# Fewer TensorE products, ScalarE marks and moved input tests in a two-layer graph attention kernel

## The chip, the cores and the metric

The kernel runs on one core of a Trainium2 chip. The metric is the device time of one execution in microseconds: 2030.03 us, the median of three runs (2026.96 to 2030.07).

## What is computed

There are 4096 nodes with 512 features and a dense 0/1 matrix `adj` (4096 x 4096). Layer 0 is attention over all pairs with 8 heads of 64; layer 1 is attention inside blocks of 128 nodes. Cut to what matters:

```
feats = einsum('nf,hfo->hno', x, W)
d = s_self[:, :, None] + s_neigh[:, None, :]
d = where(d > 0, d, 0.2 * d) * adj
x = layernorm(x + relu(softmax(d) @ feats + b))
scores = (where(mask, q @ k.T * scale, 0) + adj + adj) * where(mask, 1, -1e6)
x = layernorm(x + softmax(scores) * mask @ v)
```

`mask` is true inside a block of 128 nodes. A zero of `adj` makes the logit 0, and its exponential 1, so every pair counts in the softmax.

## The kernel before

The function `adjacency_streamed_path` does the work; `general_path` runs only if a flag computed from the inputs asks for it, and doesn't in these runs. Because the logit is a sum of a row part and a column part, exp of it is a product of vectors per node. Write E for the unmasked exponential after the leaky step, scaled by column; then A E + (1 - A) is summed against the features.

**Passes and steps.** Layer 0 goes in four passes `r` of two heads each. A pass has four chunks `c` of 1024 rows, and a chunk has 32 steps `j` of 128 columns. At a step, VectorE makes for each of the two heads a tile `q` (128 x 1024): max of a row tile and a scalar, times the adjacency tile `at` (line 1560). TensorE multiplies `q` by scaled features `g_s` into the sum `acc` (line 1607), and multiplies `at` by minus the plain features `f_s` into the sum `accf` (line 1584), in two parts of a split number: 4 matmuls for each step. From `q` a 0/1 tile `mark` is made, which tells which branch of the leaky step applied: on ScalarE by a steep sigmoid (line 1570), but for every fourth step's second head on VectorE by a comparison (line 1565). Every eight steps, TensorE sums the marks into `dens` (line 1623), from which denominators come.

**Folded steps.** `folded(j)` names steps in which A (E - 1) is made by VectorE itself, in two operations instead of one (lines 1548 and 1551), with a row `U_row` and a scalar `c_all`, its mark always on ScalarE (line 1555). Then `q` goes into `accf`, and the 4 matmuls of line 1584 fall away. In the kernel before, 36 of 512 steps are folded: 12 in pass 0, 4 in pass 1 (chunk 2), none in pass 2, 20 in pass 3.

**Groups and buffers.** In passes 0 to 2 a group is eight steps: TensorE does the group's `accf` products, then its `acc` products, then the marks' sums. Eight `q` buffers serve there (six in pass 3), so VectorE runs at most four steps ahead. At the end of a chunk `sums_to_rows` (line 1268) scales the sums on VectorE and later turns them into rows, in pieces put between groups (`run_pieces`).

**Layer 1.** In pass 3 and after it, blocks of 512 rows go through `layer_1` (line 1079), a generator that yields after each stretch of work; letters in `PLANS` and in the last line's string say which generator goes on: E the turned sums of a chunk and `rows_of_layer_0`, F the norm, R the second block's rows, a and b the two blocks in work, K the flag. Within a block: transposes to `x1T` (copied out of PSUM by ScalarE, line 1086), products to `zT` (line 1105, copied at 1112), scores (1132), exponentials on ScalarE (1157), values (1180), output products (1196), the norm and the output. `rows_of_layer_0` loads `x1b` and, per tile, `hp`, the earlier passes' output, through a pool of two buffers.

**The 0/1 tests.** `check_block` takes one of 128 tiles `ck` of `adj` (128 x 1024) through two ScalarE operations (Square, then Abs with a sum, lines 1248 and 1249), which show whether all its values are 0 or 1. The tiles have two buffers; `load_block` queues the next load on SP when one is done. They run in passes 1 to 3, one for each four steps and a second one every third time.

**What sets the order.** TensorE's order is that of the program (`manual_schedule`). The other engines' queues are ordered by the framework's planner, but for instructions pinned by `keep_in_program_order`, among them the first half of each test. [...]

Of the kernel before, what the change touches and what calls it, by code (L numbers as in the profile page):

```python
# [19 lines left out]
P = 128  # L20
# [384 lines left out]
def adjacency_streamed_path(  # L405
# [55 lines left out]

    g_d = dram.tile([PR, NT // 4, P, 4 * FP], F32, name="g_d")
    f_d = dram.tile([PR, NT // 4, P, 4 * 2 * FP], F32, name="f_d")
    FOLDED = (0, 1, PR - 1)
    FOLDS = {1: {4: (1,), 5: (0, 1), 6: (0, 1, 2)}, 2: {2: (1,), 4: (1,), 5: (0, 1), 6: (0, 1, 2)}, 3: {2: (1,), 4: (1,), 5: (0, 1), 6: (0, 1, 2)}}
    pu_d = dram.tile([3 * H, N], F32, name="pu_d")
    at_d = dram.tile([NCH, NT, P, C], F32, name="at_d")
    hs_d = dram.tile([N, FP * (PR - 1)], F32, name="hs_d")
# [468 lines left out]
        columns_of_exponentials(NB - 1, misc([P, 4, 2 * H]))  # L937

    ckp = ctx.enter_context(tc.tile_pool(name="ck", bufs=2))
    psa = ctx.enter_context(tc.tile_pool(name="ps_acc_f", bufs=1, space=PSUM))  # L940
    dens = psa.tile([P, HB], F32, name="dens")
    nc.vector.memset(dens, 0.0)
# [136 lines left out]
    def layer_1(blk, x1b, lp, lp1, lp2):  # L1079
# [91 lines left out]
        yield  # L1171
        vs = {}

        def values(u, split=FC, pv=None):
            if pv is None:
                pv, fs = misc([P, F]), range(split)
            else:
                fs = range(split, FC)
            for f in fs:
                nc.tensor.matmul(  # L1180
                    pv,
                    x1T[:, f, ts(u, P)],
                    L1["wvT"][:, f, :],
                    start=(f == 0),
                    stop=(f == FC - 1),
                )
            if fs[-1] == FC - 1:
                vs[u] = lp.tile([P, F], F32, name="v_t")
                nc.vector.tensor_add(vs[u], pv, L1["bv"])
            return pv  # L1190

        def rows_out(us):
            ys = []
            for u in us:
                po = misc([P, F])
                nc.tensor.matmul(po, pT[:, u, :], vs[u], start=True, stop=True)  # L1196
                y = lp.tile([P, F], F32, name="y_f")
                nc.vector.scalar_tensor_tensor(
                    y, po, rd[:, u : u + 1], x1b[:, u, :], op0=OP.mult, op1=OP.add
                )  # L1200
                ys.append(y)
            layernorm(ys)()
            for i, u in enumerate(us):

                queue = nc.sync if blk >= NT // 4 - 2 else nc.gpsimd
                queue.dma_start(out[ts(4 * blk + u, P), :], ys[i])

        values(0)
        pp = misc([P, 4, P])
# [8 lines left out]
        values(2)  # L1218
        if blk == NT // 4 - 1:
            last = values(3, 3)  # L1220
            rows_out((2,))
            values(3, 3, last)
            yield
            rows_out((3,))
        else:
            values(3)
            yield
            rows_out((2, 3))
# [24 lines left out]
    def rows_of_layer_0(blk, hst, lp):  # L1253
        x1b = lp.tile([P, 4, F], F32, name="x1b")
        for u in range(4):
            it = 4 * blk + u
            nc.sync.dma_start(x1b[:, u, :], x[ts(it, P), :])
            hp = lp.tile([P, F - FP], F32, name="hp_l")
            nc.sync.dma_start(hp, hs_d[ts(it, P), :])
            for dst, src in (  # L1260
                (x1b[:, u, : F - FP], hp),
                (x1b[:, u, F - FP :], hst[:, it % CT, :]),
            ):
                nc.vector.scalar_tensor_tensor(dst, src, 0.0, dst, op0=OP.max, op1=OP.add)  # L1264
        plan["F"] = layernorm([x1b[:, u, :] for u in range(4)])
        return x1b

    def sums_to_rows(r, c, acc, accf, ae, u_row, later_by):
# [178 lines left out]
    def main_pass(r, ae=None, wide=4):  # L1447
# [9 lines left out]
        for c in range(NCH):  # L1457
# [5 lines left out]
            def folded(j):  # L1463

                if r == PR - 1:
                    return r in FOLDED and c > 0 and j % 4 in FOLDS[c].get(j // 4, ())
                if r == 1:
                    return c == 2 and j in (8, 16, 24, 25)
                return r in FOLDED and j % 8 == 0 and j > 0

            def rows_for_folded():
# [32 lines left out]
                            stop=(j >= NT - 2),  # L1504
                        )

            acc = psa.tile([P, 2, HB], F32, name="acc")
            accf = psa.tile([P, 2, HB], F32, name="accf")
            marks = {}
            for j0 in range(0, NT, wide):  # L1510
# [30 lines left out]
                for j in cycle:  # L1541
                    for h in range(2):
                        hh = 2 * r + h
                        q = qs[j, h] = ring("q", qp, 6).tile([P, C], F32, name="q")
                        d_j = d_all[:, j, hh : hh + 1]
                        if folded(j):
                            cn = c_all[r][:, j, h : h + 1]
                            nc.vector.scalar_tensor_tensor(
                                q, p_row[h], d_j, U_row[h], op0=OP.max, op1=OP.mult
                            )  # L1550
                            nc.vector.scalar_tensor_tensor(  # L1551
                                q, q, cn, ats[r, c, j].bitcast(F32), op0=OP.subtract, op1=OP.mult
                            )
                            mark = marks[j, h] = sgp.tile([P, C], FP8, name="mark")
                            nc.scalar.activation(  # L1555
                                mark, q, AF.Sigmoid, bias=below_0, scale=2.0**80, saturate=False
                            )
                            continue
                        with following(at_step == 0, ("DVE", 3 if j else 2)):
                            ends_of_setup["Q"] = nc.vector.scalar_tensor_tensor(  # L1560
                                q, p_row[h], d_j, ats[r, c, j].bitcast(F32), op0=OP.max, op1=OP.mult
                            )
                        mark = marks[j, h] = sgp.tile([P, C], FP8, name="mark")
                        if j % 4 == 3 and h == 1:
                            nc.vector.tensor_scalar(  # L1565
                                mark, q, d_j, None, op0=OP.is_gt, saturate=False
                            )
                        else:
                            with following(at_step == 0, "ACT", "ROW"):
                                nc.scalar.activation(  # L1570
                                    mark,
                                    q,
                                    AF.Sigmoid,
                                    bias=nb_all[:, j, hh : hh + 1],
                                    scale=BIG,
                                    saturate=False,
                                )
# [3 lines left out]
                for j in cycle:  # L1581
                    for w in range(0 if folded(j) else 2):
                        for s in range(2):
# [4 lines left out]
                                start=(j == 0 and w == 0),  # L1588
                                stop=(j == NT - 1 and w == 1),
                            )  # L1590
                if at_step == 0:
                    columns_of_last()
                if r == 0 and (c, j0 + wide) == (NCH - 1, NT):

                    sums_over_a(c, cycle)
# [6 lines left out]
                for j in cycle:  # L1602
                    dst = accf if folded(j) else acc
                    for s in range(2):
                        for o in range(0, FP, 32):
                            h = o // FH
                            nc.tensor.matmul(  # L1607
                                dst[o : o + 32, s, :],
                                g_s[j // 4][:, j % 4, h, o % FH : o % FH + 32],
                                qs[j, h][:, ts(s, HB)],  # L1610
                                start=(j == 0),
                                stop=(j == NT - 1),
                                skip_group_check=folded(j),
                            )
                if r == 0:
                    pieces(c, j0 // 4, 1)

# [15 lines left out]
                    pieces(c, j0 // 4, 1)  # L1633
                for x_ in follow[first:]:
                    bring(*x_)
                group_0 = (at_step - NT * NCH) // 4
                for group in range(group_0, group_0 + wide // 4) if r else ():
                    if group == 0:
                        load_block()
                        load_block()  # L1640
                    for _ in range(1 + (group % 3 == 2)):
                        check_block(done[0])
                        done[0] += 1
                        load_block()
            ends.append(sums_to_rows(r, c, acc, accf, ae, u_row, 0.75 * wide))

    done = [0]
    keep = ctx.enter_context(tc.tile_pool(name="keep_f", bufs=1))
    wide_passes = ExitStack()
    more["at"], more["q"] = [(atp, 6)], [(qp, 6)]  # L1650
# [3 lines left out]
    with tc.tile_pool(name="ps_ae", bufs=1, space=PSUM) as psx:  # L1654
        ae = psx.tile([P, HB], F32, name="ae")
        nc.vector.memset(ae, 0.0)
        banks.append(psx)
        main_pass(0, ae, wide=8)
        banks.remove(psx)
    first_pass.close()  # L1660
    banks.extend([ctx.enter_context(tc.tile_pool(name="ps_misc2", bufs=2, space=PSUM))] * 2)
    with tc.tile_pool(name="wl1", bufs=1, side="right") as wp:
        pools["wl1"] = wp
        work.append(weights_of_layer_1(keep, wp))
# [4 lines left out]
            for _ in gen:  # L1669
                pass  # L1670
        work.clear()
    main_pass(2, wide=8)
    more.clear()
    wide_passes.close()
    with tc.tile_pool(name="lp", bufs=2) as lp, tc.tile_pool(
# [2 lines left out]
        pools.update(lp=lp, lp1=lp1, lp2=lp2)  # L1678
        main_pass(3)
        plan["K"] = kind_of_inputs(lp1)  # L1680
        run_plan("bbEbbFbaabRaFaKKbbababaababbbb", pinned=True)


@with_exitstack
# [50 lines left out]
```

## Time and profile before

| | |
|---|---|
| median of the runs | 2030.03 us |
| the profiled execution | 2029.65 us |
| its span, first to last instruction | 2027.9 us |
| granted TensorE clock, mean | 0.996 |
| HBM read and written over the span | 298 GB/s |
| set-up until pass 0 begins | about 156 us |
| pass 0 | to about 568 us |
| pass 1, pass 2 | to about 949 and 1327 us |
| pass 3, then the end part | to about 1891 and 2028 us |

The boundaries are the starts of the first scaling (line 1277) after a pass. A profile names an instruction by line, engine and tiles; a group's row gives busy time, the mean of one in ns, and the idle time before it with what ended it. TensorE is PE (its weight loads PEld), VectorE DVE, ScalarE ACT, GpSimd POOL, and SP the queue that issues most loads. Of the queues, SP carried 430.64 MB at 60.9% of the 16 engines' time. Over the span ScalarE waited 25.7 us for `ck` loads, 19 times, and SP's queue, in pass 3's stretch from 1430 to 1905 us, 99.6 us for ScalarE to finish tests before their buffers could be loaded again.

### The profile page before, as it was taken

Reading aid. Unit: us, or ns where it says so; the run is one execution under the profiler, and the core shown is the slowest. Engines: PE = TensorE matmul, PEld = TensorE weight load, DVE = VectorE, ACT = ScalarE, POOL = GpSimd, SP = SyncE. Lnnn points to the kernel's source line nnn. Section 1 sums busy time; section 2 is a strip of 40 time slices with the busy share of each in tenths; the row PEclk is TensorE's granted clock in tenths of the full one; section 3 lists DMA queues with packets and bytes.
Section 4 is the critical chain, followed back from the end, with each engine's and each line's share of the span. In section 5 each row is a group of like instructions: output and inputs, shape, how many; then the busy total and the mean of one; then the engine's idle time right before and its main releaser. Section 6 shows DMA issues by size and latency. Waiting matters only on the chain. (4 is left out here: it accounts for less than half of the span.)

```text
span 2027.9 us, 38096 instructions
## 1 busy us (share of the span) xinstructions
PE 1999.2 (99%) x14961; PEld 1023.0 (50%) x14961; DVE 1756.0 (87%) x2212; ACT 1524.7 (75%) x1872; POOL 231.2 (11%) x362
## 2 busy tenths in 40 slices
PE   9999999999999999999999999999999999999997
PEld 8884454545444444445445444444444444445443
DVE  5668999999999999898999999999997897899754
ACT  3348888888879898889889899999786666567420
POOL 1222222222200000000000000000020210211111
PEclk9999999999999999999999999999999999999998
DMA  6999999999999999799999899989976775775211
GB/s 210 248 328 270 296 283 277 287 292 295 323 368 342 364 343 327 257 340 310 317 318 333 304 347 334 333 280 366 320 255 197 243 246 163 233 278 161 73 55 44
DMA packets 209673, 555.74 MB, mean 274 GB/s; under 512 B 25068, under 2 KB 66412, under 8 KB 209484
## 3 DMA queue, kind: packets, MB, share of 16 engines
q1 hardware_dynamic: 145132, 430.64, 60.9%
q0 software_dynamic: 62272, 122.04, 23.4%
q8 instruction: 120, 1.97, 0.4%
q10 hardware_dynamic: 2080, 0.52, 0.1%
q14 instruction: 69, 0.57, 0.1%
HBM read 496.11 MB, written 107.35 MB: 298 GB/s over the span
## 5 line engine op out<-in xcount | busy, mean ns | idle before, releaser
L1560 DVE SCALAR_TENSOR_TENSOR q<-p_row,d_all,at 128x1024 f32<-128x1024 f32 x952 | 1154.9, 1277 | 94.2 <-PE acc L1607 38.4
L1570 ACT ACTIVATE mark<-q,nb_all 128x1024 fp8e4<-128x1024 f32 x824 | 907.6, 1148 | 137.9 <-DVE q L1560 126.9
L1607 PE MATMUL acc<-q,g_s 128*32 128x512 f32 x7616 | 841.9, 593 | 1.2 <-DVE q L1560 0.4
L1607 PEld LDWEIGHTS acc<-q,g_s 128*32 128x32 f32 x7616 | 248.5, 110 | 556.3 <-issue 495.5
L1584 PE MATMUL accf<-at,f_s 128*128 128x512 f32 x1904 | 464.3, 399 | 2.8 <-ACT at L625 2.7
L1584 PEld LDWEIGHTS accf<-at,f_s 128*128 128x128 f32 x1904 | 351.4, 189 | 109.2 <-issue 26.3
L1248 ACT ACTIVATE ck<-ck,neg_half_f 128x1024 f32<-128x1024 f32 x128 | 146.0, 1140 | 26.0 <-DMA ck<-in_adj_dram 25.7
L1249 ACT ACTIVATE ck<-ck,neg_quarter 128x1024 f32<-128x1024 f32 x128 | 146.4, 1144 | 1.9
L1555 ACT ACTIVATE mark<-q,below 128x1024 fp8e4<-128x1024 f32 x72 | 81.6, 1145 | 78.4 <-DVE q L1551 77.9
L1623 PE MATMUL dens<-mark,e_b 128*6 128x512 fp8e4 x2048 | 125.9, 379 | 1.8 <-DVE mark L1565 1.6
L807 PE MATMUL ps_fe<-w_sb_f,xT_f 128*128 128x264 f32 (+1 forms) x512 | 121.7, 395 | 1.0 <-ACT xT_f L727 1.0
L625 ACT CAST at<-ps_m 128x1024 fp32r<-128x1024 fp8e4 x124 | 117.2, 1026 | 0.0
L1180 PE MATMUL ps_m<-wvT,x1T 128*128 128x512 f32 x256 | 114.4, 594 | 0.0
L1105 PE MATMUL ps_m<-x1T,M_sb 128*128 128x512 f32 x256 | 113.0, 595 | 0.3 <-ACT x1T L1086 0.3
L807 PEld LDWEIGHTS ps_fe<-w_sb_f,xT_f 128*128 128x128 f32 x512 | 100.6, 200 | 15.7 <-ACT xT_f L727 1.8
L1371 POOL DMA_DIRECT2D hs_d<-hst x12 | 10.7, 896 | 827.6 <-DVE hst L1361 814.5
L626 POOL DMA_DIRECT2D at_d<-at x128 | 71.0, 555 | 269.9 <-ACT at L625 141.8
L1565 DVE TENSOR_SCALAR mark<-q,d_all 128x1024 fp8e4<-128x1024 f32 x128 | 95.9, 749 | 5.0 <-PE accf L1584 0.5
L1623 PEld LDWEIGHTS <-e_b 128*6 128x6 bf16 x2048 | 55.8, 86 | 79.3 <-issue 37.1
L1551 DVE SCALAR_TENSOR_TENSOR q<-q,c_all,at 128x1024 f32<-128x1024 f32 x72 | 90.5, 1274 | 0.0
L1105 PEld LDWEIGHTS ps_m<-x1T,M_sb 128*128 128x128 f32 x256 | 47.9, 190 | 59.6 <-issue 57.8
L1180 PEld LDWEIGHTS ps_m<-wvT,x1T 128*128 128x128 f32 x256 | 47.6, 190 | 56.4 <-issue 55.2
(209 smaller groups left out, 1315.3 us busy)
## 6 DMA issues: line engine op xcount, KB each, us to landing
at<-at_d SPq DMA_DIRECT2D x384, 512.0 KB, 6.0
at_d<-at POOLq DMA_DIRECT2D x128, 512.0 KB, 17.4
ck<-in_adj_dram SPq DMA_DIRECT2D x128, 512.0 KB, 5.5
f_s<-f_d SPq DMA_DIRECT2D x107, 512.0 KB, 7.5
g_s<-g_d SPq DMA_DIRECT2D x128, 256.0 KB, 5.8
f_d<-fst POOLq DMA_DIRECT2D x16, 1024.0 KB, 7.9
a_b<-in_adj_dram POOLq DMA_DIRECT2D x32, 512.0 KB, 21.1
p_row<-pu_d SPq DMA_DIRECT2D x32, 512.0 KB, 6.7
```

The costliest lines, as they stand in the source:

```text
L625: ends_of_setup["ACT"] = nc.scalar.copy(at, both[:, :, k])
L807: nc.tensor.matmul(pf[:, q, :, cols], tile_j(xTs[k][:, c].rearrange("p u n -> p (u n)"), u), w_sb[:, c, 4 * q : 4 * q + 4, cols], start=(c ...
L1105: nc.tensor.matmul(pz, L1["M"][:, f, ts(c, P)], x1T[:, f, :], start=(f == 0), stop=(f == FC - 1),)
L1180: nc.tensor.matmul(pv, x1T[:, f, ts(u, P)], L1["wvT"][:, f, :], start=(f == 0), stop=(f == FC - 1),)
L1248: tc.keep_in_program_order(nc.scalar.activation(ck, ck, AF.Square, bias=neg_half))
L1249: nc.scalar.activation(ck, ck, AF.Abs, bias=neg_quarter, accum_out=binp[:, k : k + 1])
L1560: ends_of_setup["Q"] = nc.vector.scalar_tensor_tensor(q, p_row[h], d_j, ats[r, c, j].bitcast(F32), op0=OP.max, op1=OP.mult)
L1565: nc.vector.tensor_scalar(mark, q, d_j, None, op0=OP.is_gt, saturate=False)
L1570: nc.scalar.activation(mark, q, AF.Sigmoid, bias=nb_all[:, j, hh : hh + 1], scale=BIG, saturate=False,)
L1584: nc.tensor.matmul(accf[:, s, :], f_s[j // 4][:, j % 4, w, :], ats[r, c, j][:, ts(s, HB)], start=(j == 0 and w == 0), stop=(j == NT - 1 an ...
L1607: nc.tensor.matmul(dst[o : o + 32, s, :], g_s[j // 4][:, j % 4, h, o % FH : o % FH + 32], qs[j, h][:, ts(s, HB)], start=(j == 0), stop=(j ...
L1623: nc.tensor.matmul(dens[lo : lo + 6, :], e_b[:, j, 2 * r + h, :], marks[j, h][:, ts(s, HB)], start=(j == 0), stop=(j == NT - 1),)
```

## The change

- Folded steps: 18 more, in passes 1 (14 in place of 4) and 2 (8 in place of none); each chunk there now loads its two `U_row` rows.
- Marks: in passes 1 and 2 all marks are made on ScalarE; passes 0 and 3 keep every eighth mark on VectorE.
- Tests: 20 in each of passes 1 and 2 (42 before), 63 given out in pass 3 (44), and 25 between the steps of the end part (none). A table, `CHECKS`, names how many follow each group; in the end part one or two follow each letter of the plan. The flag (K) is computed later.
- Five small moves: `columns_of_last` comes after the first `acc` products; `acc` and a scratch bank get PSUM pools of their own; `hp` of tiles 2 and 3 uses the buffers of `v_t`; the last block's norm is done in two halves; in the last block, the third tile's output product comes ahead of the end of the fourth tile's values.

```diff
-    FOLDED = (0, 1, PR - 1)
+    FOLDED = tuple(range(PR))
+    MIDDLE_FOLDS = {(1, 0): (16, 24), (1, 1): (8, 16, 24), (1, 2): (8, 9, 16, 17, 24, 25), (1, 3): (8, 16, 24)}
...
+    psq = ctx.enter_context(tc.tile_pool(name="ps_acc_q", bufs=1, space=PSUM))
+    banks.append(ctx.enter_context(tc.tile_pool(name="ps_misc1", bufs=1, space=PSUM)))
     psa = ctx.enter_context(tc.tile_pool(name="ps_acc_f", bufs=1, space=PSUM))
...
             last = values(3, 3)
+            outputs((2,))
+            values(3, 3, last, True)
             rows_out((2,))
-            values(3, 3, last)
             yield
...
-            hp = lp.tile([P, F - FP], F32, name="hp_l")
+            hp = lp.tile([P, F - FP if u < 2 else F], F32, name="hp_l" if u < 2 else "v_t")
+            hp = hp[:, : F - FP]
...
-        plan["F"] = layernorm([x1b[:, u, :] for u in range(4)])
+        n = 2 if blk == NT // 4 - 1 else 4
+        ends = [layernorm([x1b[:, u + v, :] for v in range(n)]) for u in range(0, 4, n)]
...
-                if r == 1:
-                    return c == 2 and j in (8, 16, 24, 25)
+                if r:
+                    return j in MIDDLE_FOLDS.get((r, c), (16, 24))
...
-            acc = psa.tile([P, 2, HB], F32, name="acc")
+            acc = psq.tile([P, 2, HB], F32, name="acc")
...
-                        if j % 4 == 3 and h == 1:
+                        if j % 4 == 3 and h == 1 and r in (0, PR - 1):
...
-                if at_step == 0:
-                    columns_of_last()
...
+                if at_step == 0:
+                    columns_of_last()
...
-                group_0 = (at_step - NT * NCH) // 4
-                for group in range(group_0, group_0 + wide // 4) if r else ():
-                    if group == 0:
-                        load_block()
-                        load_block()
-                    for _ in range(1 + (group % 3 == 2)):
-                        check_block(done[0])
-                        done[0] += 1
-                        load_block()
+                if at_step == NT * NCH:
+                    load_block()
+                    load_block()
+                check_blocks(CHECKS[r, c][j0 // wide] if r else 0)
...
+    CHECKS = {(1, 0): (1, 1, 1, 1), (1, 1): (1, 1, 1, 1), (1, 2): (1, 2, 1, 2), (1, 3): (1, 2, 1, 2)}
+    CHECKS.update({(2, c): (1, 1, 1, 2) for c in range(NCH)})
+    CHECKS[3, 0] = (0, 1, 1, 0, 1, 1, 0, 1)
+    CHECKS[3, 1] = CHECKS[3, 3] = (2, 2, 2, 2, 2, 2, 3, 3)
+    CHECKS[3, 2] = (2, 3, 2, 3, 3, 3, 3, 3)
+
+    def check_blocks(n):
+
+        for _ in range(min(n, N * N // (P * CK) - done[0])):
+            check_block(done[0])
+            done[0] += 1
+            load_block()
...
-        run_plan("bbEbbFbaabRaFaKKbbababaababbbb", pinned=True)
+        for k in "bbEbbFbaabRaFabbababaa":
+            run_plan(k, pinned=True)
+            check_blocks(2 if k in "EF" else 1)
+        assert done[0] == N * N // (P * CK)
+        run_plan("babKbKbb", pinned=True)
```

## The prediction

> **What bounds the kernel now.** I read the page's busy times first, then the busy times by stage, then TensorE's waits, and then the timelines of the places that the change touches.
>
> ```profile
> span 2027.9 us, 38096 instructions
> PE 1999.2 (99%) x14961; PEld 1023.0 (50%) x14961; DVE 1756.0 (87%) x2212; ACT 1524.7 (75%) x1872; POOL 231.2 (11%) x362
> ```
>
> TensorE lacks 28.7 us of the span. A busy TensorE need not be the bound, so I look at the stages (pass 1, pass 2, pass 3, and the end part from 1891 us):
>
> ```profile
> 568.00:949.00 381.00, 379.44 (x3069) 183.44 (x3062) 352.84 (x353) 330.99 (x351) 3.60 (x4) 1.00 0.94 329
> 949.00:1327.00 378.00, 378.00 (x3141) 182.41 (x3139) 350.45 (x334) 340.42 (x358) 3.54 (x4) 1.00 0.92 325
> 1327.00:1891.00 564.00, 560.66 (x3738) 266.31 (x3738) 507.27 (x673) 408.21 (x521) 70.73 (x88) 1.00 0.71 243
> 1891.00:2028.00 137.00, 121.69 (x470) 60.55 (x468) 71.85 (x180) 28.57 (x74) 20.95 (x51) 0.96 0.17 60
> ```
>
> Columns: stretch, then busy PE, PEld, DVE, ACT, POOL, granted clock, DMA share, GB/s. In passes 1 and 2 TensorE has no gap, VectorE has 7% left and ScalarE 10 to 13%. In pass 3 ScalarE has 28% left; in the end part it is nearly free, but TensorE idles there for 15 us, so that work hangs on short chains. The few waits of TensorE itself:
>
> ```profile
> PE ps_m L1085 <- DVE x1b L525: 1.8, 1, 1.8
> PE ps_m L614 <- DVE pu_all L794: 1.6, 1, 1.6
> PE dens L1623 <- DVE mark L1565: 1.6, 1, 1.6
> ```
>
> **Folded steps: the gain.** The trace of before has chunks with unfolded, once and twice folded groups of eight steps (pass 1, chunk 2), so the saving can be read from start to start:
>
> ```profile
> 761.35 7.61 PE L1584 MATMUL accf<-at,f_s 128*128 128x512 f32 x32
> 768.88 13.94 PE L1607 MATMUL acc<-q,g_s 128*32 128x512 f32 x128
> ...
> 784.48 6.68 PE L1584 MATMUL accf<-at,f_s 128*128 128x512 f32 x28
> 790.99 0.60 PE L1334 MATMUL ps_m<-ident_f,dcs 128*128 128x128 f32 x4
> ...
> 838.41 5.80 PE L1584 MATMUL accf<-at,f_s 128*128 128x512 f32 x24
> 844.05 7.03 PE L1033 MATMUL ps_m<-w_k,w_q 128*128 128x512 f32 x16
> ```
>
> 32 matmuls take 7.53 us, 28 take 6.51, 24 take 5.64: about 0.97 us less for each folded step. 18 steps more (10 in pass 1, 8 in pass 2) give 18 x 0.97 = 17.4 us, all on the path, as TensorE has no gap there. The built program's order agrees: 28 or 24 such matmuls stand in these groups where 32 or 28 stood, and nothing else changes on TensorE but two moved pieces.
>
> **What the fold and the marks cost VectorE.**
>
> ```profile
> L1560 DVE SCALAR_TENSOR_TENSOR q<-p_row,d_all,at 128x1024 f32<-128x1024 f32 x952 | 1154.9, 1277 | 94.2 <-PE acc L1607 38.4
> L1570 ACT ACTIVATE mark<-q,nb_all 128x1024 fp8e4<-128x1024 f32 x824 | 907.6, 1148 | 137.9 <-DVE q L1560 126.9
> L1565 DVE TENSOR_SCALAR mark<-q,d_all 128x1024 fp8e4<-128x1024 f32 x128 | 95.9, 749 | 5.0 <-PE accf L1584 0.5
> ...
> 1200.37 8.46 DVE L1560 SCALAR_TENSOR_TENSOR q<-p_row,d_all,at 128x1024 f32<-128x1024 f32 x7
> 1208.93 0.75 DVE L1565 TENSOR_SCALAR mark<-q,d_all 128x1024 fp8e4<-128x1024 f32 x1
> 1212.05 10.85 DVE L1560 SCALAR_TENSOR_TENSOR q<-p_row,d_all,at 128x1024 f32<-128x1024 f32 x9 [2.37 <-PE acc L1607]
> ```
>
> In a row, q's come every 1.21 us (10.85 / 9). A folded step needs two more, 2.41 us; the two marks that leave a group give 1.34 us back. So a once folded group is 1.07 us longer on VectorE and 0.97 shorter on TensorE. An ordinary group has 2.37 us idle before its fifth step, the one that waits for q buffers: 0.3 us are left, so nothing is lost. The tightest is the group at j = 8, where VectorE also turns the last chunk's sums: its idle time there is 0.93 us, plus about 0.37 us by which the last q of a group leads TensorE. In chunk 1 of pass 1 it is folded: I charge 0.6 us. In chunks 2 and 3 weights of layer 1 lengthen TensorE's groups and cover it (idle 2.8 and 3.0 us); in pass 2 j = 8 isn't folded.
>
> Here a rule speaks against the change: the Trainium skill, "ScalarE: Activation LUTs", section "Rules for kernel authors", gives simple elementwise work to VectorE, as the faster engine. The rows agree on the price (749 against 1148 ns): 64 marks cost 64 x 0.4 = 25.5 us more engine time. By the rule alone I would forecast a loss. By the stage rows VectorE is the engine without room and ScalarE gets room: 32 marks x 1.06 us (its pace in a row) = 34 us in, and in pass 2 42 checks become 20, 22 x 2.3 = 51 us out; in pass 1 the same. Its load falls to about 325 us of 370. I take the rows: no cost. Each check now stands behind a group's last mark, where the next marks have most slack.
>
> **Loads.** Passes 1 and 2 gain seven pairs of row loads (512 KB each, 7 MB) on SP's queue and lose 44 checks' loads (23 MB): no cost. A row load waits for the folded step of the chunk before, long done; the adjacency loads stand behind it.
>
> **Small moves.** The columns of the last block of exponentials (columns_of_last) put behind the first `acc` products: removes the 1.6 us wait on pu_all, but the same copy may hold a bank a little later; 1.0 of 0 to 1.6. Loading `hp` for tiles 2 and 3 into v_t's buffers: these loads no longer wait for tiles 0 and 1, so the late mark at 1656 us goes: 1.6 (0 to 1.6). PSUM pools regrouped: same number of banks, 0 (within 1 either way). The last block's norm in two halves and its y pulled forward belong to the end.
>
> **Checks in pass 3.** 62 in place of 44 there: 18 x 2.3 = 41 us into 156 us of idle ScalarE. Copies x1T and zT keep their places behind at most two checks, as some already do; TensorE's other products cover them. 0, with a bound of 5 us.
>
> **Checks in the end part: the cost.** Here no mark and no attention product is left to hide behind. ScalarE takes its queue in order; its order in the built program puts 26 checks between the copies, one half check between most of the four x1T copies of a block. A check is 2.31 us (1901.99 to 1904.30). There are two ck buffers: load k+2 starts when check k is done. The last four of them landed as in the first line below (the others show block 6's x1T copies and TensorE around them):
>
> ```profile
> DMA to landing us min/median/max: 3.7/4.5/4.6
> ...
> 1937.37 2.08 ACT L1086 COPY x1T<-ps_m 128x512 f32<-128x512 f32 x4 [12.06 <-PE ps_m L1085]
> 1938.61 1.88 PE L1196 MATMUL ps_m<-v_t,a 128*128 128x512 f32 x4
> 1940.33 13.90 PE L1105 MATMUL ps_m<-x1T,M_sb 128*128 128x512 f32 x32
> ```
>
> DMA is quieter in the end part (share 0.17), so 4.1 us, and 0.3 for the semaphores: two checks per 2.3 + 4.4 = 6.7 us. On before's clock: check 104 (counted from 0) follows the exponentials, which end at 1923.1, and ends at 1925.4; 106 starts at 1929.8, 108 at 1936.5. The first x1T copy of block 6 then ends at 1939.4, not 1937.9; check 110, between the third and fourth, waits for its load until 1943.2; the fourth ends at 1944.9. TensorE wants it at 1940.33: 4.6 us late. Next the last zT sits behind check 115 (1962.0): total shift 3.9, since the 1.8 us wait on x1b's norm is covered now. Block 7's copies have checks 116 and 117 among them; 117's load lands at 1967.6, the last copy ends at 1969.3: shift 7.7. Last, zT behind check 124 frees its PSUM bank at 1995.5, wanted at 1992.4: shift 11.1. The y pulled forward gives 0.6 back: 10.5 us net. SP's queue carries these loads too: block 7's x1b rows and the output writes stand behind ck loads that wait for ScalarE; by the same times they come 2 to 5 us later than before, still ahead of need.
>
> The skill's "DMA: Bandwidth & Descriptors", section "Anatomy of one DMA", gives 2.0 us and bytes/436e3 (fitted on GpSimd's path): 3.2 us for 512 KB, an estimate. About 12 round trips, of which nine tenths reach the end, would then take 0.9 x 12 x 0.9 = 10 us less, and the end part would cost nothing. No ck load of the trace landed in under 3.7 us in that stretch, so I stay with 4.1.
>
> **Sum**, against the profiled execution (2029.65 us, 0.4 below the median): -17.4 + 0.6 - 1.0 - 1.6 + 10.5 = -8.9, so 2020.8; I say 2021.
>
> **Rivals.** (1) *The end part hides the checks*: for it, ScalarE's 28.6 us of work in 137. Then also the 1.8 and 0.6 us go: -22 us, 2008. (2) *VectorE becomes the bound in passes 1 and 2*: its reserve in a folded group is only 0.3 us; if half the saving is eaten, 2029.5, no change. Against it: the once folded group at 816 us shows no wait. (3) *Slower: the round trip of a check's load in the end part*. At the page's median landing of 5.5 us each of 12 trips is 1.4 us longer: 0.9 x 12 x 1.4 = 15 us more, 2036. It decides from a landing of about 5.4 us, where the end part's cost passes 24 us. For it: busy stretches show 5.5 and more; against it: the DMA share of 0.17.
>
> **Numbers.** Differences over 0.2% (4 us) can be told from none. Forecast 0.48 (2013 to 2027), (1) 0.20, (2) 0.17, (3) 0.15. Faster 0.71, same 0.16, slower 0.13. Range 2008 to 2034.
>
> **What would show it.** Passes 1 and 2 shorter by 9 and 7.5 us with TensorE at 100%; pass 3 unchanged; an end part some 10 us longer, TensorE waiting there on x1T and zT copies, ScalarE on ck loads. TensorE waiting on q would be rival 2; ck landings over 5 us, rival 3; no such waits, rival 1. I am wrong if pass 3 lengthens by more than 5 us, that is if marks or adjacency loads come late there.

## The result and the profile after

The changed kernel takes 2035.34 us, the median of 20 runs (2030.19 to 2039.00); the kernel before took 2030.84 in 20 runs taken with them. The ratio is 1.0018, 95% interval [1.0011, 1.0025]: slower by about 3.7 us by the ratio (4.5 by the medians). The interval excludes 1, but by the ratio the difference is just inside the 0.2% that I had called no change. I had forecast 2021. The profiled execution took 2031.69 us with a span of 2029.9, 2.0 us more than before's span; it lies near the bottom of its kernel's runs, which matters below.

The page of the changed kernel, as before: span, then busy time by engine.

```profile
span 2029.9 us, 38082 instructions
...
PE 1990.8 (98%) x14889; PEld 1015.4 (50%) x14889; DVE 1753.2 (86%) x2187; ACT 1610.2 (79%) x1936; POOL 220.3 (11%) x364
```

TensorE has 72 matmuls and 8.4 us of busy time less, and the span is longer: it is idle for 39.1 us where it was idle for 28.7. Where, the busy times by stage show. The stages are cut here at the start of the first `acc` product of passes 1, 2 and 3 and of the last group; the columns are as in the prediction.

```profile
577.40:971.70 394.30, 387.78 (x3153) 184.41 (x3152) 365.94 (x357) 341.83 (x334) 3.59 (x4) 0.99 0.90 305
971.70:1336.10 364.40, 364.40 (x3073) 171.38 (x3072) 341.86 (x312) 328.82 (x316) 3.54 (x4) 1.00 0.89 301
1336.10:1886.10 550.00, 548.01 (x3581) 263.18 (x3580) 493.14 (x665) 430.21 (x559) 61.78 (x92) 1.00 0.76 260
1886.10:2029.90 143.80, 119.56 (x455) 59.72 (x454) 67.18 (x170) 86.48 (x151) 19.20 (x50) 0.94 0.47 152
```

Cut the same way, before had 395.0, 371.9, 551.0 and 130.3 us. So pass 2 gained 7.5 us, as forecast; pass 1 gained 0.7 in place of 9; the end part lost 13.5 in place of 10. In pass 1 and in the end part TensorE now has gaps, and the granted clock is under 1. Its largest waits name the places (total, times, longest):

```profile
PE ps_m L1036 <- DVE parts L1352: 3.7, 1, 3.7
...
PE ps_m L1088 <- DVE mv_f L519: 2.7, 1, 2.7
PE ps_m L1183 <- ACT zT L1115: 2.1, 1, 2.1
PE ps_m L1200 <- ACT x1T L1089: 2.1, 2, 1.6
...
PE ps_m L1077 <- ACT wvT L1078: 1.8, 1, 1.8
```

The first is new and stands in pass 1, chunk 2, in the group at j = 8. The timeline there, first of the kernel before:

```profile
785.92 1.28 DVE L1551 SCALAR_TENSOR_TENSOR q<-q,c_all,at 128x1024 f32<-128x1024 f32 x1
787.11 6.06 DVE L1560 SCALAR_TENSOR_TENSOR q<-p_row,d_all,at 128x1024 f32<-128x1024 f32 x5
...
790.99 0.60 PE L1334 MATMUL ps_m<-ident_f,dcs 128*128 128x128 f32 x4
...
793.09 0.31 DVE L1337 TENSOR_REDUCE parts<-ps_m 128x16 f32<-128x48 f32 x2
...
793.55 3.67 PE L1033 MATMUL ps_m<-w_k,w_q 128*128 128x512 f32 x8 [1.09 <-DVE parts L1337]
```

and then of the changed kernel:

```profile
778.90 2.47 DVE L1563 SCALAR_TENSOR_TENSOR q<-p_row,d_all,U_row 128x1024 f32<-128x1024 f32 x2
...
781.30 2.47 DVE L1566 SCALAR_TENSOR_TENSOR q<-q,c_all,at 128x1024 f32<-128x1024 f32 x2
...
783.69 4.86 DVE L1575 SCALAR_TENSOR_TENSOR q<-p_row,d_all,at 128x1024 f32<-128x1024 f32 x4
783.74 0.60 PE L1349 MATMUL ps_m<-ident_f,dcs 128*128 128x128 f32 x4
...
788.47 0.31 DVE L1352 TENSOR_REDUCE parts<-ps_m 128x16 f32<-128x48 f32 x2
...
788.93 6.23 PE L1036 MATMUL ps_m<-w_k,w_q 128*128 128x512 f32 x8 [3.72 <-DVE parts L1352]
```

The `ps_m` tiles share a few PSUM banks, which the helper `misc` hands out in turn. TensorE turns the marks' sums of the chunk before (`dcs`) into one of them, and VectorE must read it (`parts`) before the product of weights (L1036) can have it. VectorE has q's of the group in its queue ahead of `parts`. Before, the transposes ended at 791.6 and `parts` followed at 793.09. Now TensorE comes there at 783.74 and VectorE at 788.47: the fold made TensorE earlier by one set of products and VectorE later by two operations. Then the product itself takes 6.23 us in place of 3.67: the granted clock between 780 and 800 us is 0.83, from a spell of 6.83 us at half speed.

### The profile page after: what moved, and what is told of

It is laid out like the page before. It is cut to its first block, busy times and chain, and to the rows that moved or that the text cites. A ratio compares the mean times of both kernels' runs of the same rounds, so it can differ in the third digit from the quotient of the medians.

```text
span 2029.9 us, 38082 instructions
## 1 busy us (share of the span) xinstructions
PE 1990.8 (98%) x14889; PEld 1015.4 (50%) x14889; DVE 1753.2 (86%) x2187; ACT 1610.2 (79%) x1936; POOL 220.3 (11%) x364
## 3 DMA queue, kind: packets, MB, share of 16 engines
q8 instruction: 119, 1.95, 0.4%
## 4 chain that ended last, share of the span: by engine, by line
PE 76%; DVE 11%; ACT 6%; DMA 3%; issue 3%; SPq 0%; POOL 0%; DVEq 0%; POOLq 0%; ACTq 0%
PE acc L1620 31%; PE accf L1599 17%; DVE q L1575 6%; PE ps_fe L808 5%; PE accf L1620 4%; PE ps_m L1183 4%; PE dens L1638 4%; PE ps_m L1108 3%; DMA ck<-in_adj_dram 2%; DVE q L1566 2%; ACT mark L1585 1%; DVE q L1563 1%; ACT at L626 1%; PE ps_m L1135 1%; ACT ck L1256 1%
## 5 line engine op out<-in xcount | busy, mean ns | idle before, releaser
L1575 DVE SCALAR_TENSOR_TENSOR q<-p_row,d_all,at 128x1024 f32<-128x1024 f32 x916 | 1110.7, 1276 | 90.0 <-ACT mark L1585 28.8
L1585 ACT ACTIVATE mark<-q,nb_all 128x1024 fp8e4<-128x1024 f32 x852 | 948.4, 1151 | 134.6 <-DVE q L1575 116.4
L1620 PE MATMUL acc<-q,g_s 128*32 128x512 f32 x7328 | 813.8, 593 | 1.0
L1620 PEld LDWEIGHTS acc<-q,g_s 128*32 128x32 f32 x7328 | 242.1, 110 | 540.9 <-issue 478.4
L1599 PE MATMUL accf<-at,f_s 128*128 128x512 f32 x1832 | 446.1, 398 | 0.8 <-ACT at L626 0.6
L1599 PEld LDWEIGHTS accf<-at,f_s 128*128 128x128 f32 x1832 | 336.7, 188 | 103.3 <-issue 25.9
L1570 ACT ACTIVATE mark<-q,below 128x1024 fp8e4<-128x1024 f32 x108 | 122.6, 1147 | 77.2 <-DVE q L1566 75.2
L1566 DVE SCALAR_TENSOR_TENSOR q<-q,c_all,at 128x1024 f32<-128x1024 f32 x108 | 134.9, 1276 | 0.0
L1620 PE MATMUL accf<-q,g_s 128*32 128x512 f32 x864 | 101.2, 596 | 0.0
L1563 DVE SCALAR_TENSOR_TENSOR q<-p_row,d_all,U_row 128x1024 f32<-128x1024 f32 x64 | 79.9, 1276 | 0.0
```

Source lines behind the costliest of these rows:

```text
L1566: nc.vector.scalar_tensor_tensor(q, q, cn, ats[r, c, j].bitcast(F32), op0=OP.subtract, op1=OP.mult)
L1575: ends_of_setup["Q"] = nc.vector.scalar_tensor_tensor(q, p_row[h], d_j, ats[r, c, j].bitcast(F32), op0=OP.max, op1=OP.mult)
L1585: nc.scalar.activation(mark, q, AF.Sigmoid, bias=nb_all[:, j, hh : hh + 1], scale=BIG, saturate=False,)
L1599: nc.tensor.matmul(accf[:, s, :], f_s[j // 4][:, j % 4, w, :], ats[r, c, j][:, ts(s, HB)], start=(j == 0 and w == 0), stop=(j == NT - 1 an ...
L1620: nc.tensor.matmul(dst[o : o + 32, s, :], g_s[j // 4][:, j % 4, h, o % FH : o % FH + 32], qs[j, h][:, ts(s, HB)], start=(j == 0), stop=(j ...
```

## The experiments

My theory after reading the two traces: the folds gain what I gave them, the five small moves too; one group in pass 1 loses 5 us to VectorE's order, and the tests lose 13 in the end part. The main rival: the small moves make the end part long, and the tests are hidden there. Times are medians against the kernel before on the same chip, with the ratio's 95% interval; part lengths are cut as above, from each run's profile.

**Tests where they were** (`e1`). The folds, the marks and the small moves stay.

```diff
+    for g in range(32 * (PR - 1)):
...
+        CHECKS.setdefault((r, c), []).append(1 + (g % 3 == 2))
...
-        for k in "bbEbbFbaabRaFabbababaa":
-            run_plan(k, pinned=True)
-            check_blocks(2 if k in "EF" else 1)
-        run_plan("babKbKbb", pinned=True)
+        run_plan("bbEbbFbaabRaFabbababaababKbKbb", pinned=True)
```

> The changed kernel with the tests handed out as before: 42 in pass 1, 43 in passes 2 and 3, none in the end part; folds, ScalarE marks and small moves kept. Theory (the folds gain as sized; the 25 tests in the end part cost it 12 to 13.5 us): about 2035.3 - 13 = 2022 us, with an end part of about 130 us. ScalarE is nearly full then in passes 1 and 2 (331 + 34 = 365 us of about 372), so up to 8 us could be lost again there: 2022 to 2030. Rival (the end part is long because of the small moves, the norm in halves and the output product pulled forward, not because of the tests): end part still about 142 us, time 2034 or more.

2022.98 us, ratio 0.9965 [0.9952, 0.9979], end part 129.2 us. The theory holds, and the rival falls. But pass 2 is back at 372.6 us: the folds gain nothing there.

```profile
968.80:1341.40 372.60, 367.50 (x3073) 172.18 (x3072) 342.03 (x312) 357.73 (x380) 3.54 (x4) 1.00 0.90 325
...
PE dens L1638 <- ACT mark L1585: 5.1, 8, 0.7
```

ScalarE (the fourth pair) is busy for 357.7 of 372.6 us, and TensorE waits for its marks there 8 times, 5.1 us in all. So moving all marks to ScalarE did force tests out of pass 2: its load was counted in the prediction, but not that the place of the tests depends on it.

**The 25 tests of the end part in pass 3** (`e2`), 88 there, passes 1 and 2 as in the change.

```diff
-    CHECKS[3, 0] = (0, 1, 1, 0, 1, 1, 0, 1)
-    CHECKS[3, 1] = CHECKS[3, 3] = (2, 2, 2, 2, 2, 2, 3, 3)
-    CHECKS[3, 2] = (2, 3, 2, 3, 3, 3, 3, 3)
+    CHECKS[3, 0] = (1, 1, 1, 1, 1, 1, 1, 2)
+    CHECKS[3, 1] = CHECKS[3, 3] = (3, 3, 3, 3, 3, 3, 3, 4)
+    CHECKS[3, 2] = (3, 4, 3, 4, 4, 4, 3, 4)
```

> The changed kernel with the 25 tests of the end part given to pass 3 (88 there), nothing else changed. Theory (tests cost only where nothing covers them): pass 3's ScalarE goes from about 450 to 508 us of 564 and still covers them, the end part falls to about 130 us: 2022 us. Rival 1 (a test costs TensorE about half a microsecond wherever layer 1 runs, since x1T and zT copies queue behind it): pass 3 grows by about 13 us, 2034. Rival 2 (small moves lengthen the end part): 2035.

2044.46 us, ratio 1.0063 [1.0045, 1.0082]: my theory missed by 22 us, and rival 1 named the mechanism at half its size. The end part is 130.9 us, pass 3 is 578.6 in place of 550: more than one microsecond for each test, although ScalarE is busy for only 480 of those 579 us. TensorE is idle for 18.4 us there (2.0 in the changed kernel), and five spells at half clock, 20.5 us long together, cost up to 10 more. The longest wait, first ScalarE's queue, then TensorE's:

```profile
1722.51 1.15 ACT L1255 ACTIVATE ck<-ck,neg_half_f 128x1024 f32<-128x1024 f32 x1 [1.06 <-DMA ck<-in_adj_dram]
1723.56 1.13 ACT L1570 ACTIVATE mark<-q,below 128x1024 fp8e4<-128x1024 f32 x1
1724.60 1.13 ACT L1256 ACTIVATE ck<-ck,neg_quarter 128x1024 f32<-128x1024 f32 x1
...
1725.73 2.17 ACT L1570 ACTIVATE mark<-q,below 128x1024 fp8e4<-128x1024 f32 x2
1727.81 0.56 ACT L1219 COPY a<-ps_m 128x512 f32<-128x512 f32 x1
...
1728.42 3.00 PE L1108 MATMUL ps_m<-x1T,M_sb 128*128 128x512 f32 x4 [3.18 <-ACT a L1219]
```

A copy that TensorE needs (`a`, 0.56 us) stands behind two halves of a test, three marks and a wait for a load. Idle time elsewhere in the pass does not help this copy.

**One fold less** (`e3`): the fold of step 9 in chunk 2 of pass 1 goes.

```diff
-(1, 2): (8, 9, 16, 17, 24, 25)
+(1, 2): (8, 16, 17, 24, 25)
```

> The changed kernel without the fold of step 9 in chunk 2 of pass 1 (17 more folds than before, not 18). Theory (the two folds of that group put three more VectorE operations ahead of the sums of the chunk before, TensorE waits 3.7 us for them and then runs at half clock for 6.8 us): the group gets about 5.2 us back and pays 1.0 for the step: 2031.3 us. Rival (VectorE's time in the chunk sets the group anyway, the wait only moves): 2035 to 2036.5.

2031.74 us, ratio 1.0000 [0.9991, 1.0010]: 3.6 us under the changed kernel's median (3.0 if each is taken against the kernel before on its own chip), with one fold fewer. Pass 1 is 391.1 us, 3.2 less. The clock is 1.00 from 780 to 800 us, and the wait of TensorE on `parts` there is 0.4 us.

**Only the tests moved** (`e4`): the kernel before with the table `CHECKS` and the new end of the plan, nothing else.

> The kernel before with only the tests moved: table of the changed kernel, 25 tests in the end part; folds, marks and small moves as before. Theory (tests in the end part cost 12 to 13.5 us there, and their leaving the middle passes gains nothing): 2030.8 + 12.5 = 2043 us, end part about 143 us. Rival (small moves make the end part longer): 2031 us, end part about 131 us.

2043.56 us, ratio 1.0065 [1.0051, 1.0079]; the end part is 143.0 us, passes 1 to 3 are within 0.7 us of before. The tests' move alone costs some 13 us, nearly all at the end.

**Tests in pass 1** (`f1`): 42, 20 and 66 tests in the passes, none in the end part, and the fold of step 9 left out.

> The changed kernel with 42 tests in pass 1, 20 in pass 2, 66 in pass 3 (8 in its first chunk), none in the end part, and without the fold of step 9 in chunk 2 of pass 1. Theory (tests are free in pass 1 and in chunk 0 of pass 3, not in pass 2, in pass 3's layer-1 groups beyond two or three, or in the end part): after's 2035.3 - 13.5 for the end part - 4.3 for the group in chunk 2 + 0.7 for pass 1 = 2018 us, faster than both kernels. Rival (a full ScalarE in pass 1 delays marks once its groups are shortened by folds): 2022 to 2025, with waits for marks in pass 1.

2017.25 us, ratio 0.9941 [0.9926, 0.9956], as forecast. Pass 1 is 396.4 us, 5.3 more than e3's 391.1 with the same folds and 20 tests: ScalarE's room ends there too (TensorE waits 2.6 us for marks), which I had put at 0.7.

**The end part's tests without their loads** (`f2`). It leaves out the loads of the last 25 tiles, so these tests are not made on their data.

```diff
+        if per * NT > k >= per * NT - 25:
+            checked.append(checked[k - 2])
```

> The changed kernel whose last 25 tests read a tile that is already there again: it leaves out the loads of these 25 tiles, so these tests are not made on their data. ScalarE does the same operations in the same order. Theory as in the prediction (the round trip of a test's load sets ScalarE's pace in the end part, and so holds the copies): ScalarE no longer waits for loads, end part 133 to 136 us instead of 143.8, time 2026 to 2028. Rival (ScalarE's own time, 25 x 2.3 us put between the copies, is the cost): end part 141 us or more, time 2033 or more.

2028.34 us, ratio 0.9991 [0.9981, 1.0000]; the end part is 141.5 us. The time is what the prediction's mechanism asked for, the length of the end part is not. With no load to wait for, TensorE still waits for copies behind ScalarE's own work, in other places, and two spells at half clock fall into this profile's end part:

```profile
PE ps_m L1200 <- ACT x1T L1089: 2.6, 2, 2.0
PE ps_m L1088 <- ACT x1T L1089: 2.4, 2, 2.0
...
1886.90:2028.40 141.50, 122.26 (x455) 61.64 (x454) 67.14 (x170) 84.73 (x151) 19.57 (x50) 0.92 0.18 61
```

**Marks back on VectorE** (`f3`): every eighth mark of passes 1 and 2.

```diff
-                        if j % 4 == 3 and h == 1 and r in (0, PR - 1):
+                        if j % 4 == 3 and h == 1:
```

> The changed kernel with every eighth mark of passes 1 and 2 back on VectorE. Theory (a folded group has only 0.3 us of VectorE time to spare, and the two marks are 1.34 us a group): a folded group is bound by VectorE and its fold gains nothing or little: pass 2 goes from 364.4 back to 371 or more, pass 1 up by 4 to 8 us, 2043 to 2050 in all. Rival (VectorE has room, the marks' move is not needed): 2035, pass 2 at 364.4.

2049.17 us, ratio 1.0094 [1.0077, 1.0112]. Pass 1 is 403.9 us, pass 2 is 369.8, with VectorE busy for 363.2 of it and TensorE, by the records, for all of it. Yet the same matmuls take 5.4 us longer than in the changed kernel. In the kernel before, VectorE waited in pass 2 for buffers that TensorE frees:

```profile
DVE q L1560 <- PE acc L1607: 14.5, 11, 2.5
```

In f3 no such wait is left: VectorE is the late one. "TensorE 100% busy" is no proof that it sets the time. Pass 2 came just under the 371 us or more of the forecast, and pass 1 lost 9.6 us where 4 to 8 were forecast.

**The small moves alone** (`f4`): folds, marks and tests as before.

> The five small moves alone: folds, marks and tests as in the kernel before. Theory (waits on pu_all and hp go, 1 to 2 us each; the end part is 1 us shorter, as in the kernel with the tests as before): about 2030.5 - 4 = 2026.5 us. Rival (the moves cost something in the end part or in set-up): 2031 or more.

2021.97 us, ratio 0.9965 [0.9952, 0.9978]: 7.6 us faster, where I had 4. Set-up and pass 0 give 1.7 us, pass 3 gives 3.7 and the end part 1.6. Pass 3's part is more than the wait of 1.6 us at 1656 us that I had counted; 1.1 us of it, in chunk 1 at j = 16, came in e4 too, where only the tests moved, so not all of it is `hp`'s. The five moves were not tried one by one.

**Only the loads** (`g2`). The two ScalarE operations of the last 25 tests are replaced by a GpSimd operation on one column; it leaves these tests out.

> The changed kernel in which the last 25 tests are loaded as there, but not made: a small GpSimd operation takes the first column of each tile in place of the two ScalarE operations. It leaves out the test of 25 tiles. Theory after the run without loads (ScalarE's own 25 x 2.3 us in its queue between the copies are the cost, not the loads): end part 129 to 131 us, time about 2021. Rival (the loads on SP's queue delay the end part's own loads and writes, or the DMA's traffic does): end part 134 us or more, 2026.

2033.76 us, ratio 1.0018 [1.0010, 1.0025], end part 144.1 us. The run is inconclusive: GpSimd works on the norms too, in order, and its stand-in waited up to 13.9 us for a load ahead of them. Two more runs follow.

**Loads from ScalarE's queue** (`h1`) take SP out, **tests of one column** (`h2`) take most of ScalarE's time out; h2 leaves out the test of the other 1023 columns of 25 tiles.

```diff
+            queue = nc.scalar if k >= per * NT - 23 else nc.sync
-            ins = nc.sync.dma_start(ck, ...)
+            ins = queue.dma_start(ck, ...)
```

```diff
+        if k >= N // CK * NT - 25:
+            ck = ck[:, :1]
```

> The changed kernel with the last 23 loads of test tiles issued from ScalarE's own queue, behind the test that frees the buffer, in place of SP's queue, where x1b's loads and the output writes stand behind them. Theory A (ScalarE's own time in the end part is enough to cost 12 us, as the run without loads showed): end part 141 us or more. Theory B (the end part's loads standing behind the tests' loads on SP is what costs): end part 135 us or less.

> The changed kernel whose last 25 tests are made on the first column of each tile only: it leaves out the test of the other 1023 columns. Loads, their queue and ScalarE's waits for them stay; ScalarE's work falls from 25 x 2.3 us to about 25 x 0.6. Theory A (ScalarE's time is the cost, and the 144 us of the run with loads alone came from GpSimd's queue, where the stand-in waited for loads ahead of the norms' operations): end part 133 us or less, time about 2023. Theory B (loads and waits for them are enough by themselves to hold the copies and x1b): end part 138 us or more.

h1: 2039.48 us, ratio 1.0036 [1.0024, 1.0047], end part 152.0. h2: 2031.44 us, ratio 1.0003 [0.9995, 1.0012], end part 142.0. In h2 ScalarE waits for loads in place of working: 30.0 us in 16 waits, where the changed kernel waited 13.7 us in that stretch.

Moving the loads off SP makes it worse. With the small moves alone (f4), and in h2, the end parts read:

```profile
1892.10:2020.80 128.70, 115.33 (x455) 57.80 (x454) 66.77 (x170) 27.89 (x73) 19.44 (x50) 0.96 0.19 64
...
1887.60:2029.70 142.10, 118.93 (x455) 59.96 (x454) 66.76 (x170) 45.75 (x151) 19.14 (x50) 0.94 0.46 153
```

TensorE's idle time there (the stretch less its busy time) is 13.4 us in f4 and 24.2 in the changed kernel. Of these 10.8 us that came with the tests, 9.8 stay with the loads and a third of ScalarE's added work (h2), and 5.8 with all of ScalarE's work and no loads (f2), each in one profile. The two spells at half clock, against one in the changed kernel, hide most of f2's gain. By the medians, each against the kernel before on its own chip, f2 gives back 5.8 us and h2 3.7. So neither alone gives the end part back: the loads keep most of the waiting, ScalarE's work about half, and the two overlap.

The loads act in a way that my theories had left out: other transfers land later. The loads of `x1b` in the end part took 6.3 us in the median, where they took 3.7 before and 4.5 in f4. The wait at 1948.5 us, TensorE's longest there, is not for a copy behind a test, but for the norm of `x1b`. Ahead of that norm VectorE had stood still, until 1944.0, for an output write that took 6.2 us to land. VectorE's waits for transfers in the end part of the changed kernel:

```profile
DVE x1b L1272 <- DMA x1b<-in_x_dram: 6.8, 4, 4.8
...
DVE y_f L1122 <- DMA out_dram<-y_f: 4.0, 1, 4.0
```

Six profiles with such loads on SP's queue (the changed kernel, g3, e3, e4, f3, h2) have a wait for an output write, of 2.6 to 4.1 us; none without these loads has one. In f2 and f4 the waits for `x1b` are 3.6 and 2.4 us. In h2 TensorE waits 3.7 us for the norm of `x1b` and 4.3 for a copy. No run takes this path out alone, so what it is worth stays open.

**Tests and marks where there is room** (`g1`). No test in the end part; in passes 1 and 2 marks wholly on ScalarE only in folded groups, which carry two tests (two of them three); unfolded ones carry three. The fold of step 9 is left out.

```diff
-                        if j % 4 == 3 and h == 1 and r in (0, PR - 1):
+                        if j % 4 == 3 and h == 1 and (r in (0, PR - 1) or not any(map(folded, cycle))):
```

> The changed kernel with no test in the end part and marks on ScalarE only where a group is folded; unfolded groups of passes 1 and 2 keep two marks on VectorE and carry three tests, folded ones two (39 and 40 tests in passes 1 and 2, 49 in pass 3); fold of step 9 in chunk 2 of pass 1 left out. Theory (an unfolded group has 2.4 us of VectorE time to spare and a folded one about 5 us of ScalarE's, so folds, marks and tests fit if each goes where its engine has room): from the kernel before -7.6 for the small moves, -7.5 for pass 2, about -6 for pass 1: 2009 us. Rival (ScalarE's sum over the pass is what counts, about 355 of 364 us and queued in order, so marks come late): pass 2 at 369 to 372 us, 2015 to 2020.

2012.28 us, ratio 0.9908 [0.9891, 0.9924]: the fastest version, 18.4 us under the kernel before, though 3 short of the 2009 forecast. Its passes 1 and 2:

```profile
576.10:967.80 391.70, 387.14 (x3157) 182.86 (x3156) 370.35 (x365) 359.63 (x381) 3.60 (x4) 1.00 0.93 331
967.80:1332.30 364.50, 364.50 (x3077) 171.45 (x3078) 352.95 (x329) 341.14 (x359) 3.55 (x4) 1.00 0.92 331
```

Pass 2 keeps its whole gain with 40 tests, twice the change's: VectorE has 11 us more work than in the changed kernel and ScalarE 12, each in groups that have room for it.

**The changed kernel again** (`g3`), for a second profile.

> The changed kernel once more, for a second profile. Its runs spread over 2030 to 2039 us and the first profile is of a run near the bottom. Theory (the spread is half-clock spells of TensorE after waits of about 2 us or more, whose number changes from run to run): the waits are the same to 0.5 us, and a slower run shows more or longer spells. Rival (waits themselves change in length): stages differ by more than their spells account for.

2037.2 us, span 2035.4. Pass 3 is 4.1 us longer and the end part 3.1. The waits of the end part are the same to about 0.5 us, but half-clock spells follow at 1935.3 and 1989.9 us where the first profile has none. In pass 3 a wait itself changed: near 1704 us TensorE waits 2.1 us for the copy `a` where it waited 0.5, because ScalarE waits 1.95 us for a test's load where it waited 0.33, and a spell follows at 1706.6. The three spells of 3.4 us at half speed (1.7 us each) and the 1.6 us of that wait make 6.7 of the 7.2 us. So the theory holds for the end part, and both the theory and its rival for pass 3.

## Why the prediction was wrong, step by step

Two steps failed. The larger is the gain of the folds in pass 1: with the 0.6 us charged for VectorE, 9.1 us were forecast and 0.7 came (points 1 to 3). The other is the cost of the tests: 11.1 us were forecast at the end and none in pass 3, and 15.1 and 2.6 came, in g3 18.2 and 6.7 (points 6 and 7). The half clock after waits, in no term of the sum, enlarges both.

1. *18 folds at 0.97 us each.* Right where nothing else is in the way: 0.89 to 1.02 us in each of pass 2's eight folded groups, 7.5 us in all. (The three lengths in the prediction give 0.945; over 18 folds that is 0.4 us.) In pass 1 the ten folds bring 0.7 us net; points 2 and 3 say where the rest went.
2. *VectorE's lag of 0.6 us in chunk 1 of pass 1.* Right: the two groups around it gain 1.28 us in place of 1.9.
3. *"In chunks 2 and 3 weights of layer 1 lengthen TensorE's groups and cover it."* This step failed. I compared VectorE's load with the group's length and did not look at the order: the weights' products themselves wait for a bank that VectorE must read first, and VectorE comes to it only behind two folded steps and four more q's. In chunk 2 that costs 5.2 us (2.6 of wait and 2.6 of half clock; without the second fold, in e3, the wait is gone). In chunk 3 the fold at j = 8 gains only 0.15, and with a wait of 1.8 us for the copy of wvT (L1077) the last group is 2.0 us off. That wait came with every kernel that has the added folds, with marks back on VectorE too (f3, g1); the causes in chunk 3 were not tried and stay open.
4. *Marks on ScalarE at no cost.* Right in passes 1 and 2 with 20 tests each, and needed: without the move the folds lose 14 us (f3). The rule on such work that the prediction cited would have made it worse. But the price is hidden in the tests, which for that had to leave (e1), and g1, which follows the rule in unfolded groups, is better than both, though part of its lead is that no test stands in the end part.
5. *Small moves, 2.6 us without the end part's.* Right in direction and too small: f4 gives 7.6 in all.
6. *62 tests in pass 3 at 0.* Off by 2.6 us in the profiled execution (549.9 against 547.3 in f4). In seven other profiles with the same pass 3 (e3, f2, f3, g2, g3, h1, h2) it is 3.6 to 6.7, in four of them beyond my bound of 5. e2 shows that the next 25 cost 28.7.
7. *The end part, +11.1 for the tests.* 143.8 against 128.7 us in f4: 15.1. I made the sum from the loads' round trip; its landings came at 3.7 to 6.0 us, mostly under 4, so my 4.1 was good, and the 3.2 worked out from the page's fit too low. But the round trip is not all of it: without loads, ScalarE's work alone left about half of the waiting (f2). The step "still ahead of need" failed: an output write, late to land, held VectorE for 4 us, and TensorE waited 2.7 us for `x1b`'s norm at 1948.5. After that wait it ran at half speed for 6.83 us, some 3 us that no term of mine had.

In the profiled execution: folds -8.2, small moves -7.0, tests +2.6 and +15.1, some -0.5 in set-up that changes from run to run: +2.0 in place of -8.9. The median run is 3.7 us slower than this one; g3, slower still, shows such time in spells and in a wait for a load. Rival 3, slower at 2036, gives nearly the time that came, but by luck: the tests' loads landed after 3.9 us in the median, not 5.4 (the x1b loads and output writes were the ones that came late).

## What to carry to other kernels

An engine's idle time over a stage says little on what an added operation costs: ask which instruction stands behind it in that engine's queue, who waits for that, and how soon. Faster work on the engine that sets the time makes it meet the others earlier; at each point where it takes back a buffer, compare the two orders, not the two loads. Work that only has to be done at some time belongs in stretches where its engine's next result has slack, and group by group: g1 makes the same marks and tests in other places, with one fold fewer, and takes 23 us less than the change.

## What the hardware showed

The granted clock often halves after a wait. In the 15 profiles, from 150 us to the last 30 us, 31 of 35 gaps of TensorE over 2 us were followed within some 4 us by a spell at 0.50 of the clock, and 12 of 51 gaps of 1 to 2 us. Of the 42 spells, 4 followed no single gap over 1 us, but two or three of 0.4 to 0.9 us close together. All but one last 3.41 or 6.83 us, one or two units of the same length; the other is three. Pass 1's group in the changed kernel (clock 0.83, third number from the end), for one:

```profile
780.00:800.00 20.00, 16.28 (x86) 8.20 (x88) 13.74 (x19) 11.84 (x13) 0.89 (x1) 0.83 0.60 199
```

The Trainium skill, "TensorE: Matmul & The Clock Gate", section "What's actually happening", describes a free-running window of 3413 ns and a slow state after an idle one; the length of the spells agrees. An idle stretch of a whole window was not needed here: waits of 2.04 us already were followed by a spell. And the same wait of 2.1 to 2.2 us near 1704 us was followed by a spell in some runs (e3, g3, h1, h2) and by none in f2. Where a spell follows and TensorE has work, it costs up to 1.7 us (3.41 at half speed) or 3.4 us (6.83) beyond the wait. The time also spreads from run to run: the kernels without such waits (f4, g1) had a clock of 0.996 to 0.998 in their runs, the changed kernel 0.991 to 0.994.
